# A graph layer's row gathers: two of every eight get 126 rows in place of 125

## The chip, the cores and the metric

The kernel runs on one core of a Trainium2 chip. The metric is the time of one execution on the device in microseconds (us), lower is better. A core has five engines that run their own instruction lists side by side: PE (matrix multiply), DVE (vector), ACT (scalar functions), POOL (general purpose, here the one that issues the gathers) and SP (issues plain transfers). Sixteen DMA engines move the data.

## What is computed

One message-passing layer over a graph with 12500 nodes of 64 features and 412500 edges (both directions of 200000 drawn pairs, and a loop at each node), sorted by receiver. Cut to what matters:

```python
h = relu(layernorm(x))
msg_in    = concat([h[src], h[dst], edge_attr_32], -1)      # 64 + 64 + 32
messages  = swish(msg_in @ W1 + b1) @ W2 + b2
logits    = swish(msg_in @ Wa1 + ba1) @ Wa2 + ba2
messages *= softmax(logits, axis=0)                         # over all edges
agg = segment_sum(messages, dst, num_segments=12500)
out = x + swish(concat([h, agg], -1) @ Wu1 + bu1) @ Wu2 + bu2
```

## The kernel before

**Tables.** The products of the sender's part with the two first weight matrices are made once for every node and written to a table in device memory, `ts_d`, with 128 floats (512 bytes) a node. A second table `tr_d` holds the receiver's part. An edge then needs one row of `ts_d`, by its sender's number, and no matrix product for it.

**Tiles and groups.** Edges are worked in tiles of `EP = 125`, one edge a partition, and in groups of `K = 8` tiles; there are `T = 3304` tiles and `NG = 413` groups. The senders' numbers lie in `src_full`, 128 partitions by 3304 tiles, of which partitions 125 to 127 hold zeros; `src_sb` is its first 125 partitions.

**The gather.** `load(g)` (L523) takes a buffer `gs` of 128 partitions by 8 tiles by 128 floats from a pool of seven and issues one indirect DMA on POOL for each tile (L529 to L532): partition p gets the row of `ts_d` whose number stands in `src_sb[p, tile]`. In the 131 groups in `chosen` (every third one from group 10 on, but for the last twelve) the eighth tile is not gathered; ACT copies its columns one by one out of an SBUF copy (L503). That leaves 3304 - 131 = 3173 gathers. The same `load` issues the loads of the receivers' window (`wins`, on SP), of edge features and receivers' numbers (`eo`, `dbs`, on SP), the comparison on DVE that makes a one-hot matrix (L555), and four matrix products on PE that give the receiver's and the edge's part, `pe` (L559).

**The rest of a group.** `begin(g)` (L567) adds `pe` and the gathered rows on DVE (L570; it reads all gathered tiles of the group at once) and lets ACT take the tanh (L573). `end(g)` makes the message and the logit on DVE (L583 to L594), `by_node` weighs and sums the messages by receiver with DVE (L637) and PE (L643), and `put` adds the sums to a running table (L668 to L675). The softmax is kept as a running maximum with factors.

**Order.** The loop over groups (L735) runs `begin(g)`, then `load(g + 2)`, then `end(g)`, so that gathers run two groups ahead in the list; what is marked with `pin` keeps its written order on its engine. POOL issues nothing but gathers in this loop. Each gather's list entry waits for the gather eight before it (one of eight completion counters in turn), and the first of a group also for the engines that last read its buffer.

Of the kernel before, what the change touches and what calls it, by code (L numbers as in the profile page):

```python
# [44 lines left out]
F32 = mybir.dt.float32  # L45
# [8 lines left out]
P = 128  # L54
EP = 125
# [3 lines left out]
C = 2 * U  # L59
S1 = U + 1  # L60
K = 8
# [13 lines left out]
PHASE = 1  # L75
SLOTS = (((0, 24), (24, 24)), ((48, 24), (72, 12)), ((84, 24), (108, 17)))
ROUND = 12582912.0
EPS = 1e-5
NEG = -3.0e38
BIG = 3.0e38  # L80
# [9 lines left out]
def gnn_kernel(ctx: ExitStack, tc: tile.TileContext, n_edges, x, src, src_row, dst, dst_row, first, edge,  # L90
# [73 lines left out]
    with tc.tile_pool(name="node1", bufs=1) as node1, \  # L164
# [41 lines left out]
        eps = node1.tile([P, 1], F32, name="eps")  # L206
        nc.vector.memset(eps, EPS)
        pin(nc.scalar.activation(node1.tile([P, 1], F32, name="spare"), eps, AF.Sqrt))
# [90 lines left out]
        for c, nn in chunks:  # L299
            tr = node.tile([P, CB, C], F32, name="tr")[:, :nn, :]  # L300
            for b in range(0, nn, 4):
                n = min(4, nn - b)
                pn = node_ps.tile([P, 4, C], F32, name="pn", bufs=4)
                for i in range(0, n, 2):
# [7 lines left out]
        pin(nc.scalar.dma_start(hT_d, hT))  # L312

    one_pass(tc, n_edges, locals())
    again = nc.values_load(wrong[0:1, 0:1], min_val=0, max_val=1,
                           skip_runtime_bounds_check_because="it is the outcome of a comparison")
# [76 lines left out]
def one_pass(tc, n_edges, v):  # L393
    nc = tc.nc
    NB, T, NG, NP, NT = (v[k] for k in ("NB", "T", "NG", "NP", "NT"))
    ident, iota_w, bj, dloc, src_sb, base_sb, real, unreal, far, wrong = (
        v[k] for k in ("ident", "iota_w", "bj", "dloc", "src_sb", "base_sb", "real", "unreal",
                       "far", "wrong"))
    ts_d, tr_d, bq_d, xb_d, edge, dst_row = (
        v[k] for k in ("ts_d", "tr_d", "bq_d", "xb_d", "edge", "dst_row"))  # L400
    wa2, ba2_c, w2b, wu1a, wu2h, we, gather = (
        v[k] for k in ("wa2", "ba2_c", "w2b", "wu1a", "wu2h", "we", "gather"))
# [8 lines left out]
    with ExitStack() as ctx:  # L411
# [38 lines left out]
        for w in wins:  # L450
            nc.vector.memset(w, 0.0)
            for r in range(2):
                rows = slice(WR + r * DE, WR + (r + 1) * DE)
                nc.vector.tensor_copy(w[rows, :, r, :], we[rows, None, :].to_broadcast([DE, 2, C]))
        with tc.tile_pool(name="work2", bufs=2) as work2, \
# [3 lines left out]
            pes, gss, lgs, ps_, psums, sps, pps, ees, mts, nums, cols = ({} for _ in range(11))  # L459
# [20 lines left out]
            def places(g):  # L480
# [7 lines left out]
                pin(nc.vector.tensor_scalar(near, to, 1.0 / m, 0.5 / m - 0.5, op0=ALU.mult, op1=ALU.add))  # L488
                pin(nc.vector.tensor_scalar(near, near, ROUND, None, op0=ALU.add))
                pin(nc.vector.tensor_scalar(near, near, ROUND, float(1 - m * P), op0=ALU.subtract, op1=ALU.mult))  # L490
                pin(nc.vector.scalar_tensor_tensor(to, to, float(P), near, op0=ALU.mult, op1=ALU.add))
# [13 lines left out]
            def burst(g, k):  # L505
                for i in range(EVERY):
# [6 lines left out]
                           ap=[[C, NP + WR - SHIFT], [SHIFT * C, 2], [1, C]])  # L513

            def registers(g, engine, at, base=base_sb, top=NP - 1):
                n = min(NQ, NG + (base is not base_sb) - g)
                _, regs = nc.values_load_multi_w_load_instructions(
                    base[0:1, g:g + n], engines=[engine], min_val=0, max_val=top,
                    skip_runtime_bounds_check_because=WHY)
                for i in range(n):  # L520
                    at[g + i] = regs[i]

            def load(g):  # L523

                t = g * K
                if g % NQ == 0:
                    registers(g, ENG.SP, at_sp)
                gs = gss[g] = gather.tile([P, K, C], F32, name="gs")[:EP]
                for j in range(K - (g in chosen)):  # L529
                    nc.gpsimd.indirect_dma_start(  # L530
                        out=gs[:, j, :], out_offset=None, in_=ts_d[:, :],
                        in_offset=bass.IndirectOffsetOnAxis(ap=src_sb[:, t + j:t + j + 1], axis=0))  # L532
                if g % NQ == 0:
                    n = min(NQ, NG - g) * E2
                    eo = eos[g // NQ % 2]
                    i = g // NQ % 2
                    db = dbs[i * WR:(i + 1) * WR].bitcast(I32)
                    for i in range(g, min(g + NQ, NG)):
                        e = slice((i - g) * E2, (i - g + 1) * E2)
                        ees[i] = eo[:, e], db[:, e]  # L540
                    nc.sync.dma_start(eo[WR:, :n],
                                      edge[:, g * E2:g * E2 + n])
                    for r in range(2):
                        nc.sync.dma_start(
                            db[r * R:(r + 1) * R, :n],
                            bass.AP(tensor=dst_row.tensor, offset=dst_row[r:r + 1, g * E2:].offset,
                                    ap=[[0, R], [1, n]]))
                eo, db = ees.pop(g)
                win = wins[g % WINS]
                for r in range(2):  # L550
                    nc.sync.dma_start(win[r * R:(r + 1) * R, :, r, :],
                                      tr_w[bass.ds(at_sp[g], R), :, :])
                for h in range(2):
                    e = slice(h * E2 // 2, (h + 1) * E2 // 2)
                    pin(nc.vector.tensor_scalar(eo[:WR, e], db[:, e], bj[g // NQ % 2 * WR:(g // NQ % 2 + 1) * WR, g, h:h + 1], None,  # L555
                                                op0=ALU.is_equal))
                pe = pes[g] = pre_ps.tile([P, K, C], F32, name="pe")[:EP]
                for q in range(H):
                    pin(nc.tensor.matmul(pe[:, 2 * q:2 * q + 2, :], eo[:, q * EP:(q + 1) * EP],  # L559
                                         win[:, q // 2, :, :], start=True,  # L560
                                         stop=q < H - 1 or g not in chosen))
                if g in chosen:
                    to, _ = cols[g]
                    pin(nc.vector.scalar_tensor_tensor(to, nums[g], half, to, op0=ALU.is_equal, op1=ALU.mult))
                    pin(nc.tensor.matmul(pe[:, K - 1, :], to, stack, start=False, stop=True))
# [166 lines left out]
            for g in range(AHEAD):  # L732
                load(g)
            done = 0
            for g in range(NG):  # L735
# [18 lines left out]
                if g + AHEAD < NG:  # L754
                    load(g + AHEAD)
# [382 lines left out]
```

## Time and profile before

| What | Value |
|---|---|
| median of 3 runs (lowest, highest) | 4922.53 us (4922.45, 4923.75) |
| the profiled execution's own time | 4935.06 us |
| its span, first to last instruction | 4933.3 us |
| mean granted clock of PE | 0.611 |
| gathers: number, busy, idle before them | 3173, 3853.9 us, 1020.6 us |
| DMA engines, mean busy share in mid-run | 0.33 to 0.34 |

The profile is a record of one execution. It gives each engine's busy time, and for each group of instructions (by line of the kernel) how often it ran, its mean length and what ended the idle time before it. A name behind an arrow is what the instruction waited for; "issue" is time in which it waited for nothing that the profile shows. For a gather POOL counts as busy while it prepares the transfer, not while the data move. The records of the DMA engines list every packet with its queue, size and duration; POOL's gathers are queue q0.

### The profile page before, as it was taken

The numbers are of one execution on the slowest core, as the hardware profiler recorded it, in microseconds if no ns is written. First come the engines' busy times: TensorE is split into PE (matmuls) and PEld (weight loads), VectorE is DVE, ScalarE is ACT, GpSimd is POOL, SyncE is SP. The second block draws the span as 40 slices with busy tenths as digits, with TensorE's granted clock in tenths as the row PEclk, the third lists the DMA queues.
The fourth block names the chain that finished last, engine by engine and source line by source line (L and its number), as shares of the span: only waits on it lengthen the run. The fifth ranks groups of instructions, "written<-read, shape, count | busy, mean of one in ns | idle before, by whom it ended". The sixth has DMA issues, their size and how long they took to land. (4 is left out here: it accounts for less than half of the span.)

```text
span 4933.3 us, 81829 instructions
## 1 busy us (share of the span) xinstructions
PE 2429.9 (49%) x11509; PEld 1950.7 (40%) x11509; DVE 3456.5 (70%) x9793; ACT 2214.0 (45%) x17625; POOL 3871.1 (78%) x3198
## 2 busy tenths in 40 slices
PE   5455555445544444544444544444445445444455
PEld 4343344334433333433333443333334334334344
DVE  6677777777776766766766776766767667667667
ACT  3444444444444444444444444444444444444412
POOL 4777877777777777777777777777777777777775
PEclk8666655665666665555665555566566666655655
DMA  7333333333333333333333333233333333333333
GB/s 248 76 76 83 87 75 82 89 74 83 81 75 76 71 74 76 70 75 76 69 76 76 68 76 76 68 76 76 69 76 71 74 76 70 75 76 70 75 91 81
DMA packets 377225, 396.20 MB, mean 80 GB/s; under 512 B 230333, under 2 KB 306039, under 8 KB 376290
## 3 DMA queue, kind: packets, MB, share of 16 engines
q0 software_dynamic: 253840, 206.77, 19.0%
q1 hardware_dynamic: 121458, 174.49, 14.9%
q10 hardware_dynamic: 1376, 9.67, 0.5%
q14 instruction: 457, 3.74, 0.3%
q8 instruction: 94, 1.54, 0.1%
HBM read 361.41 MB, written 25.72 MB: 78 GB/s over the span
## 5 line engine op out<-in xcount | busy, mean ns | idle before, releaser
L530 POOL DMA_INDIRECT gs<-ts_d,src_sb x3173 | 3853.9, 1215 | 1020.6 <-issue 962.4
L559 PE MATMUL pe<-wins,eo 128*125 128x256 f32 x3304 | 1524.4, 637 | 1551.2 <-DVE eo L555 1288.7
L503 ACT COPY cols<-hT 128x1 f32 x16375 | 1630.2, 189 | 754.3 <-issue 749.8
L559 PEld LDWEIGHTS pe<-wins,eo 128*125 128x125 f32 x3304 | 997.4, 319 | 1872.4 <-DVE eo L555 1375.5
L570 DVE TENSOR_TENSOR gs<-pe,gs 125x1024 f32<-125x1024 f32 (+1 forms) x413 | 487.5, 1180 | 1153.1 <-DMA gs<-ts_d,src_sb 1140.2
L573 ACT ACTIVATE pe<-gs 125x1024 f32<-125x1024 f32 x413 | 424.8, 1029 | 1768.2 <-DVE gs L570 859.2
L637 DVE TENSOR_SCALAR wt<-iota_w,dloc,p 125x40 f32<-125x40 f32 x3304 | 772.5, 364 | 1.8
L643 PE MATMUL sp<-wt,acts 125*65 125x40 f32 x6608 | 652.2, 270 | 13.2 <-DVE wt L637 9.2
L643 PEld LDWEIGHTS sp<-wt,acts 125*65 125x65 f32 x6608 | 612.5, 185 | 23.6 <-DVE wt L637 14.0
L613 PE MATMUL mt<-ident,mx 125*128 125x125 f32 x110 | 48.1, 438 | 644.7 <-DVE sums L672 608.1
L654 PEld LDWEIGHTS mt<-ss,w2u 65*128 65x128 f32 x826 | 210.7, 283 | 362.0 <-issue 235.4
L654 PE MATMUL mt<-ss,w2u 65*128 65x40 f32 x826 | 188.3, 322 | 262.8 <-DVE gm L620 199.4
L555 DVE TENSOR_SCALAR eo<-dbs,bj 64x250 f32<-64x250 int32 x826 | 303.2, 397 | 17.9 <-DMA dbs<-in_dst_row_dram 8.5
L591 DVE TENSOR_TENSOR pe<-pe,w_all 125x512 f32<-125x512 f32 x413 | 288.8, 699 | 13.7
L589 DVE SCALAR_TENSOR_TENSOR pe<-pe,gs 125x512 f32<-125x512 f32 x413 | 287.4, 696 | 10.8
L583 DVE SCALAR_TENSOR_TENSOR acts<-pe,gs 125x512 f32<-125x512 f32 x413 | 284.6, 689 | 12.8 <-issue 2.4
L594 DVE TENSOR_REDUCE lg<-pe 125x8 f32<-125x512 f32 x413 | 284.2, 688 | 10.8
L613 PEld LDWEIGHTS mt<-ident,mx 125*128 125x128 f32 x110 | 20.0, 182 | 655.8 <-issue 652.2
L675 DVE COPY stand<-nmax 64x40 f32 x826 | 217.1, 263 | 3.3
L672 DVE TENSOR_TENSOR sums<-sums,mt 64x40 f32 x606 | 114.4, 189 | 4.7 <-issue 0.4
L668 DVE SCALAR_TENSOR_TENSOR sums<-sums,scale,mt 64x40 f32 x220 | 55.8, 254 | 78.4 <-PE mt L654 59.6
L356 DVE TENSOR_SCALAR bu<-mt,w_all 64x256 f32<-64x256 f32 (+1 forms) x50 | 23.9, 478 | 92.6 <-PE mt L347 78.6
(124 smaller groups left out, 1123.2 us busy)
## 6 DMA issues: line engine op xcount, KB each, us to landing
eo<-in_edge_dram SPq DMA_DIRECT2D x103, 500.0 KB
dbs<-in_dst_row_dram SPq DMA_DIRECT2D x206, 250.0 KB
gs<-ts_d,src_sb POOLq DMA_INDIRECT x3173
wins<-tr_d SPq DMA_DIRECT2D x826, 32.0 KB
num<-in_src_row_dram SPq DMA_DIRECT2D x131, 62.5 KB
ts_d<-ts SPq DMA_DIRECT2D x5, 896.0 KB
tr_d<-tr ACTq DMA_DIRECT2D x5, 896.0 KB
hT_d<-hT ACTq DMA_DIRECT2D x1, 3136.0 KB
```

The source lines that it names most:

```text
L503: pin(nc.scalar.copy(to[:, first + i:first + i + 1], hT[:, bass.ds(regs[i], 1)]))
L530: nc.gpsimd.indirect_dma_start(out=gs[:, j, :], out_offset=None, in_=ts_d[:, :], in_offset=bass.IndirectOffsetOnAxis(ap=src_sb[:, t + j:t ...
L555: pin(nc.vector.tensor_scalar(eo[:WR, e], db[:, e], bj[g // NQ % 2 * WR:(g // NQ % 2 + 1) * WR, g, h:h + 1], None, op0=ALU.is_equal))
L559: pin(nc.tensor.matmul(pe[:, 2 * q:2 * q + 2, :], eo[:, q * EP:(q + 1) * EP], win[:, q // 2, :, :], start=True, stop=q < H - 1 or g not in ...
L570: pin(nc.vector.tensor_tensor(gss[g][:, :n, :], pes[g][:, :n, :], gss[g][:, :n, :], ALU.add))
L573: pin(nc.scalar.activation(pes[g], gss[g], AF.Tanh))
L583: pin(nc.vector.scalar_tensor_tensor(acts[g % ACTS][:, :, 0:U], th[:, :, U:C], 1.0, gs[:, :, U:C], op0=ALU.add, op1=ALU.mult))
L589: pin(nc.vector.scalar_tensor_tensor(att, th[:, :, 0:U], 1.0, gs[:, :, 0:U], op0=ALU.add, op1=ALU.mult))
L591: pin(nc.vector.tensor_tensor(att, att, wa2[:EP, None, :].to_broadcast([EP, K, U]), ALU.mult))
L637: pin(nc.vector.tensor_scalar(wt[:, j, :], iota_w[:EP, j // H, :], dloc[:, g * K + j:g * K + j + 1], p[:, k + j:k + j + 1], op0=ALU.is_equ ...
L643: pin(nc.tensor.matmul(sp, acts[g % ACTS][:, j, :], wt[:, j, :], start=j == 0, stop=j == K - 1))
L654: pin(nc.tensor.matmul(pp, w2u.rearrange("s h u -> s (h u)"), sps.pop(g), start=True, stop=True))
```

## The change

In each group the tiles j = 2 and j = 3 are gathered with 126 rows. The destination is 126 partitions of the buffer's 128, and the index list is 126 partitions of `src_full`; the 126th index is one of the zeros, so row 0 of `ts_d` goes to partition 125, which no instruction reads. The six other gathers of a group (five in a chosen one) keep their 125 rows. Everything else reads the first 125 partitions as before.

```diff
+WIDE = 126
...
-                gs = gss[g] = gather.tile([P, K, C], F32, name="gs")[:EP]
+                full = gather.tile([P, K, C], F32, name="gs")
+                gs = gss[g] = full[:EP]
                 for j in range(K - (g in chosen)):
+                    rows = WIDE if j in (2, 3) else EP
                     nc.gpsimd.indirect_dma_start(
-                        out=gs[:, j, :], out_offset=None, in_=ts_d[:, :],
-                        in_offset=bass.IndirectOffsetOnAxis(ap=src_sb[:, t + j:t + j + 1], axis=0))
+                        out=full[:rows, j, :], out_offset=None, in_=ts_d[:, :],
+                        in_offset=bass.IndirectOffsetOnAxis(ap=src_full[:rows, t + j:t + j + 1], axis=0))
```

In the changed kernel these lines stand three further down (L533 for the gather).

More of the change, by code (lines that the diff above doesn't have):

```diff
@@ L395, in one_pass @@
     NB, T, NG, NP, NT = (v[k] for k in ("NB", "T", "NG", "NP", "NT"))
-    ident, iota_w, bj, dloc, src_sb, base_sb, real, unreal, far, wrong = (
-        v[k] for k in ("ident", "iota_w", "bj", "dloc", "src_sb", "base_sb", "real", "unreal",
+    ident, iota_w, bj, dloc, src_full, base_sb, real, unreal, far, wrong = (
+        v[k] for k in ("ident", "iota_w", "bj", "dloc", "src_full", "base_sb", "real", "unreal",
                        "far", "wrong"))
```

## The prediction

> **What bounds the kernel now.** I read the page's busy shares and slices first, then the waits, then the gather's own line, then a stretch of the time line. The page's chain of work is no help here: it follows back only the last 0.1 us. Busy time by engine (share of the span, number of instructions) and POOL's row of the 40 slices:
>
> ```profile
> PE 2429.9 (49%) x11509; PEld 1950.7 (40%) x11509; DVE 3456.5 (70%) x9793; ACT 2214.0 (45%) x17625; POOL 3871.1 (78%) x3198
> ...
> POOL 4777877777777777777777777777777777777775
> ```
>
> POOL is busiest, and evenly so, yet 22% is missing. The waits say who waits for whom (us in total, times, longest):
>
> ```profile
> PEld pe L559 <- DVE eo L555: 1375.5, 381, 10.6
> ...
> DVE gs L570 <- DMA gs<-ts_d,src_sb: 1140.2, 303, 7.9
> POOL gs L530 <- issue: 962.4, 2993, 49.5
> ACT pe L573 <- DVE gs L570: 859.2, 199, 12.2
> ```
>
> PE and ACT wait for DVE, DVE waits for the gathers' data, and the gathers wait for nothing in the program ("issue"). The time line shows how (start, length, idle before it):
>
> ```profile
> 2997.52 1.21 POOL L530 DMA_INDIRECT gs<-ts_d,src_sb  x1 [0.30 <-issue]
> 2999.04 1.21 POOL L530 DMA_INDIRECT gs<-ts_d,src_sb  x1 [0.30 <-issue]
> 3000.55 1.21 POOL L530 DMA_INDIRECT gs<-ts_d,src_sb  x1 [0.30 <-issue]
> ```
>
> A metronome: 1.21 us of work and 0.30 us between two instructions, 1.52 us a gather. The line's own totals (lengths in ns, then what ended the idle time before it, in us and times, and last who waited for it):
>
> ```profile
> L530 POOL DMA_INDIRECT gs<-ts_d,src_sb x3173: 1207/1212/1726, 51.9 to 4875.7; - x199
> ...
>   issue: 962.4, 2993
> ...
>   DMA gs<-ts_d,src_sb: 7.5, 14
> ...
>   DVE gs L570: 1142.3, 304
> ```
>
> First start 51.9, last end 4875.7 + 1.2 = 4876.9, so 4825.0 us of the 4933.3 are this line: 3853.9 busy and some 971 between instructions (its 1020.6 idle less 49.5 before the first). Only 14 gathers ever waited for a landing (7.5 us in all), so free buffers and slow transfers are not the limit. Before lie 51.9 us, behind 56.4 us, and the change touches neither. The time of this kernel is 3173 gathers times 1.52 us plus 108 us.
>
> **The change, part by part.** Instruction counts and waits are the same on all five engines; on PE, DVE, ACT and SP the lists agree row for row. The two gathers j = 2 and 3 of each of the 413 groups get 126 rows. No chosen group drops them (those drop j = 7), so 826 gathers change and 2347 do not.
>
> Edits that cost nothing: partition 125 of the gather buffer is written and read by nobody. The index array already holds 128 partitions and was already loaded whole, so no load is added. The 512 bytes more are 826 x 512 B = 0.42 MB on a queue that moves 206.77 MB, in DMA engines busy a third of the time; without that cover they would be 826 times the 27 ns that a 512-byte packet takes in the trace, 22 us over all engines. No wait is added, so nothing new queues behind a gather. An earlier landing of tiles 2 and 3 is worth nothing either, since DVE's addition (L570) reads all tiles of the group, and the last ones keep 125 rows.
>
> What can cost or pay is POOL's own time on a 126-row gather. No row of this trace has one, so I look at what a 125-row gather leaves behind:
>
> ```profile
> q0 software_dynamic: 253840, 206.77, 19.0%
> ```
>
> That is 253840/3173 = exactly 80 packets a gather. By size the trace's records have 15 of 4096 B, 5 of 512 B, 33 of 32 B and 27 of 4 B for each. The 20 large ones are 5 x (3 x 8 + 1) = 125 rows: five of the 16 engines get 25 rows each. The small ones are, for the 11 other engines, 3 x 8 + 1 = 25 entries of 4 B, plus 16 completions. So every one of 16 rings is filled 26 entries deep, 11 of them with dummies. The split is even, into five, and five is the largest number up to 16 that divides 125. Read the same way 126 goes to 14 engines with 9 rows, and the rings are 10 deep: 16 levels fewer.
>
> [...]
>
> What is a level worth? POOL's other instructions bound it (count, busy us, mean ns):
>
> ```profile
> L840 POOL TENSOR_TENSOR gs<-gs,eo 128x512 f32<-128x512 f32 x6 | 7.6, 1270 | 24.4 <-ACT mt L827 20.2 <-DVE gs L835 2.5 <-issue 1.7
> ...
> L141 POOL IOTA iota_p<- 32x1 f32 x4 | 0.5, 127 | 0.1
> ...
> masks.py:197 POOL MEMSET ident<- 128x128 f32 x1 | 0.2, 205 | 0.3 <-POOLq L1130 0.3
> ...
> L1130 POOL MEMSET const-float32-1.0<- 128x1 f32 x1 | 0.1, 102 | 0.0
> ```
>
> Least: a level is one element column of a memset, (205 - 102)/127 = 0.81 ns, and 16 levels are 13 ns. Most: an instruction's fixed part is the 127 ns of the smallest iota and all the rest is levels: (1212 - 127) x 16/26 = 668 ns. [...] I take 179 ns; it is nearest to work that POOL really does, and it leaves 1.03 us a wide gather. The 0.30 us between instructions I leave as it is.
>
> Sum, on the profiled execution's own span: 826 x 0.179 = 148 us less, 4933.3 - 148 = 4785. That execution took 4935.06 us (span and 1.8 around it) against a median of 4922.53, so in terms of the median 4785 x 4922.53/4933.3 = **4775 us**, 3.0% faster. The stall does not reappear within that: a group's period falls from 8 x 1.517 = 12.1 us (less in chosen groups) by 0.36, and the stretch 2000 to 3000 us has DVE 692.56 busy, so DVE would stand at 71%.
>
> [...]
>
> **The rivals.** (B) Slower: engines that carry data are what costs, not levels. Place: the same 826 instructions, whose live engines go from 5 to 14. Bounds for one live engine: 10 ns, from the first packets of a gather's 16 rings, which start within some 0.16 us of each other, and (1212 - 127)/5 = 217 ns if nothing else costs. It decides from 179/9 = 20 ns an engine, where it eats the gain. Its geometric middle, 47 ns, gives 9 x 47 - 179 = +244 ns, x 826 = +201 us, **5123 us**. For it: data packets rise from 20 to 28, and a dummy needs no index. Against it: the dummies are written all the same, in the same depth, as if 16 rings were filled side by side.
>
> (C) Nothing: rows cost, one by one, however they are split (or the split stays as it is and the change does no more than it says). 1212/125 = 9.7 ns a row, x 826 = +8 us, **4931 us**, +0.16%. For it: the simplest reading of a loop over an index list. Against it: 291 of 416 entries are not rows.
>
> (D) The gain nears the upper end, 668 ns, and another engine becomes the bound. 826 x 0.668 = 552 us would leave 4371; DVE's 3456.5 us busy would then be 79% and its waits for PE and ACT would show. I hold anything below 4640 (342 ns saved, half the most) at 8 in 100.
>
> **How the numbers follow.** A 0.46 (0.08 of it below 4640), B 0.42 (0.10 of it above 5130), C 0.12 (a measurement of this kernel tells 0.2% from no change; most of C is within that, 0.09, the rest slower). The time is A's, 4775; A's own range is 4640 to 4900. As the signs share the chance, the range spans 4640 to 5130 and leaves out 0.18. Faster 0.46, within 0.2% 0.09, slower 0.45.
>
> **What would show it.** Split: q0 should have 2347 x 80 + 826 x 48 = 227408 packets (14 x 2 data, 2 x 2 dummies, 16 completions); near 253840 the split is another and A and B both fall. Price: in the gather's line the median stays 1212 and 826 instructions, two adjacent ones in every eight, stand at some 1030 ns (A), 1450 (B) or 1222 (C). End: first start near 51.9 and a tail near 56 us; if the gathers then wait for something other than "issue", POOL has stopped being the bound and D holds. Wrong would be a gap that moves off 0.30 us, or unchanged gathers that change too.

## The result, and the profile after

The changed kernel takes 4744.97 us (median of 4 runs, 4742.4 to 4745.24) against 4922.49 us before (4 runs): a ratio of 0.9638, 95% interval 0.9621 to 0.9654. It is 177.5 us faster; forecast were 4775 us.

The page of the changed kernel, its busy times, POOL's row of slices and POOL's transfer queue (packets, MB, share of 16 engines):

```profile
PE 2412.1 (51%) x11509; PEld 1935.5 (41%) x11509; DVE 3391.0 (71%) x9793; ACT 2202.3 (46%) x17625; POOL 3682.4 (78%) x3198
...
POOL 4777777777777777777777777777777777777775
...
q0 software_dynamic: 227408, 206.34, 19.4%
```

Every engine has the same number of instructions as before, and POOL has 188.7 us less to do. Queue q0 has exactly the 227408 packets that follow from 14 equal shares of 9 rows. By size, with 80 packets for each of the 2347 other gathers, they leave 14 of 4096 B, 14 of 512 B, 2 of 32 B and 18 of 4 B for each wide one. The gathers' own line (lengths in ns, first and last start, then what ended the idle time before it):

```profile
L533 POOL DMA_INDIRECT gs<-ts_d,src_sb x3173: 992/1209/1550, 52.2 to 4685.9; - x199
...
  issue: 952.1, 2961
...
  DMA gs<-ts_d,src_sb: 15.1, 40
```

The first gather starts where it did (52.2 us) and the tail is as long (last end 4687.1, span 4742.9: 55.8 us). Between them lie 4635.0 us, 190.0 less than before. The time line of a group in mid-run (start, length, idle before it):

```profile
2994.23 1.21 POOL L533 DMA_INDIRECT gs<-ts_d,src_sb  x1 [0.30 <-issue]
2995.74 1.00 POOL L533 DMA_INDIRECT gs<-ts_d,src_sb  x1 [0.30 <-issue]
2997.05 1.00 POOL L533 DMA_INDIRECT gs<-ts_d,src_sb  x1 [0.30 <-issue]
2998.35 1.21 POOL L533 DMA_INDIRECT gs<-ts_d,src_sb  x1 [0.30 <-issue]
```

Two adjacent gathers are 0.21 us shorter, the gap stays at 0.30 us, and still nothing but POOL itself sets the pace. By tile the medians are 996 ns for j = 2 and 3 and 1209 ns for the six others. And who waits for whom (us in total, times, longest):

```profile
PEld pe L562 <- DVE eo L558: 1283.1, 378, 11.1
...
DVE gs L573 <- DMA gs<-ts_d,src_sb: 1006.7, 289, 8.6
POOL gs L533 <- issue: 952.1, 2961, 49.8
ACT pe L576 <- DVE gs L573: 829.1, 212, 11.7
```

Beside the lines of before, the two waits on DVE and the wait on the gathers' data have all shrunk, by 30 to 134 us, as is to be expected when POOL delivers sooner; none has taken the place of another.

### The profile page after: what moved, and what is told of

Its sections match the earlier page's. It is cut to its first block, busy times and chain, and to the rows that moved or that the text cites. A ratio compares the mean times of both kernels' runs of the same rounds, so it can differ in the third digit from the quotient of the medians.

```text
span 4742.9 us, 81829 instructions
## 1 busy us (share of the span) xinstructions
PE 2412.1 (51%) x11509; PEld 1935.5 (41%) x11509; DVE 3391.0 (71%) x9793; ACT 2202.3 (46%) x17625; POOL 3682.4 (78%) x3198
## 3 DMA queue, kind: packets, MB, share of 16 engines
q0 software_dynamic: 227408, 206.34, 19.4%
## 5 line engine op out<-in xcount | busy, mean ns | idle before, releaser
L533 POOL DMA_INDIRECT gs<-ts_d,src_sb x3173 | 3665.2, 1155 | 1019.6 <-issue 952.1
L646 PE MATMUL sp<-wt,acts 125*65 125x40 f32 x6608 | 641.2, 267 | 12.9 <-DVE wt L640 10.6
L646 PEld LDWEIGHTS sp<-wt,acts 125*65 125x65 f32 x6608 | 600.1, 182 | 24.2 <-DVE wt L640 19.9
L594 DVE TENSOR_TENSOR pe<-pe,w_all 125x512 f32<-125x512 f32 x413 | 288.7, 699 | 13.7
L558 DVE TENSOR_SCALAR eo<-dbs,bj 64x250 f32<-64x250 int32 x826 | 281.0, 370 | 17.8 <-DMA dbs<-in_dst_row_dram 8.5
L678 DVE COPY stand<-nmax 64x40 f32 x826 | 185.4, 224 | 3.3
L675 DVE TENSOR_TENSOR sums<-sums,mt 64x40 f32 x606 | 114.1, 188 | 4.6 <-PE mt L657 0.6
```

What stands on the lines that cost most here:

```text
L533: nc.gpsimd.indirect_dma_start(out=full[:rows, j, :], out_offset=None, in_=ts_d[:, :], in_offset=bass.IndirectOffsetOnAxis(ap=src_full[:ro ...
L594: pin(nc.vector.tensor_tensor(att, att, wa2[:EP, None, :].to_broadcast([EP, K, U]), ALU.mult))
L646: pin(nc.tensor.matmul(sp, acts[g % ACTS][:, j, :], wt[:, j, :], start=j == 0, stop=j == K - 1))
```

## The experiments

The words are the prediction's, and they are a reading of packet counts. A gather of 125 rows leaves 15 packets of 4096 B, 5 of 512 B, 33 of 32 B and 27 of 4 B, and the counter that it completes on is stepped 16 times (at the changed kernel's first gather, one of 125 rows, 11 times within 0.17 us, and five times 0.65 us and more after those). Read as 16 rings, one for each DMA engine: five hold 25 rows each, eight to a large packet; 11 hold as many dummies of 4 B, eight to a packet of 32 B; each ends in one entry more. Depth is counted below without that last entry, and an engine with data is an equal share of the rows. The records name neither an engine nor an entry; measured are the packets, the steps and POOL's times. The theory: POOL pays for each entry of the deepest ring (a level). Its rivals: it pays for dummies, for packets, for rows, or for engines that carry data; or a shape costs something by what stands beside it. All ratios are against the kernel before on the same chip.

### Sixteen row counts in one run (e1_shapes)

```diff
+SHAPES = (125, 126, 128, 127, 124, 122, 120, 112, 110, 100, 96, 80, 64, 50, 25, 16)
...
+    junk = const.tile([P, C], F32, name="junk")
...
+                if 8 <= g < NG - 13:
+                    rows = SHAPES[g % len(SHAPES)]
+                    nc.gpsimd.indirect_dma_start(
+                        out=v["junk"][:rows], out_offset=None, in_=ts_d[:, :],
+                        in_offset=bass.IndirectOffsetOnAxis(ap=v["src_full"][:rows, t:t + 1], axis=0))
```

> The kernel before, with one gather more in most groups, into a buffer that nobody reads; its row count goes in turn through 125, 126, 128, 127, 124, 122, 120, 112, 110, 100, 96, 80, 64, 50, 25, 16. Only the length of these gathers on POOL is of interest (the time grows by some 380 gathers). Depth theory (13.5 ns for each entry of the deepest ring, 216 ns/16, whoever carries data): 128 and 120 rows 982 ns, 112 969, 110 and 100 1009, 96 955, 80, 50 and 25 all 942, 64 928, 16 888, 124 1293, 122 1698, 127 2589. Dummy theory (0.84 ns for each dummy entry, 216/257, no price on depth): 128, 112, 96, 80, 64 and 16 all 981, 120 988, 110 1023, 100 1031, 50 1006, 25 1027, 124 1293, 122 1698, 127 2581. Packet theory (108 ns for every started eight entries of a ring): everything with up to 8 entries 888, 110 and 100 996, 124 1212, 122 1644, 127 2508. Row theory (9.7 ns a row): 16 rows 155, 64 rows 621, 127 rows 1231.

The scheduler moved these extra gathers forward (they run from 140 to 2235 us), and most (306 of 392) wait for the one before to land, as they write one buffer. So this run's time (6199.11 us) says nothing; the lengths do. POOL's time line over five of them, which by their order in the list take 126, 128, 127, 124 and 122 rows:

```profile
1050.19 1.00 POOL L537 DMA_INDIRECT junk<-ts_d,src_sb  x1 [2.42 <-DMA junk<-ts_d,src_sb]
1053.52 0.96 POOL L537 DMA_INDIRECT junk<-ts_d,src_sb  x1 [2.33 <-DMA junk<-ts_d,src_sb]
1056.41 2.55 POOL L537 DMA_INDIRECT junk<-ts_d,src_sb  x1 [1.93 <-DMA junk<-ts_d,src_sb]
1064.58 1.30 POOL L537 DMA_INDIRECT junk<-ts_d,src_sb  x1 [5.61 <-DMA junk<-ts_d,src_sb]
1068.47 1.67 POOL L537 DMA_INDIRECT junk<-ts_d,src_sb  x1 [2.60 <-DMA junk<-ts_d,src_sb]
```

127 rows take 2.55 us where 126 take 1.00 and 128 take 0.96. And two pairs that matter below, of 110 and 100 rows, then of 25 and 50:

```profile
1003.95 1.01 POOL L537 DMA_INDIRECT junk<-ts_d,src_sb  x1 [0.30 <-issue]
1007.47 1.01 POOL L537 DMA_INDIRECT junk<-ts_d,src_sb  x1 [2.51 <-DMA junk<-ts_d,src_sb]
...
1030.61 0.95 POOL L537 DMA_INDIRECT junk<-ts_d,src_sb  x1 [1.79 <-DMA junk<-ts_d,src_sb]
...
1289.60 0.94 POOL L537 DMA_INDIRECT junk<-ts_d,src_sb  x1 [0.31 <-issue]
```

The medians of the 24 or 25 gathers of each shape, with the number of equal shares, worked out as the largest divisor up to 16, and the rows in each share:

| rows | shares | rows in each | ns |
|---|---|---|---|
| 127 | 1 | 127 | 2556 |
| 122 | 2 | 61 | 1671 |
| 124 | 4 | 31 | 1298 |
| 125 | 5 | 25 | 1214.5 |
| 110 | 11 | 10 | 1012 |
| 100 | 10 | 10 | 1012 |
| 126 | 14 | 9 | 999 |
| 120 | 15 | 8 | 991 |
| 50 | 10 | 5 | 950 |
| 25 | 5 | 5 | 951 |
| 128 | 16 | 8 | 958 |
| 112 | 16 | 7 | 943 |
| 96 | 16 | 6 | 932 |
| 80 | 16 | 5 | 919 |
| 64 | 16 | 4 | 912 |
| 16 | 16 | 1 | 870 |

The trace's packet count agrees with the two middle columns: with them, at eight rows or dummies a packet at most, dummies to the same depth in the rings without rows and one packet more at the end of each ring, the 392 extra gathers leave 24480 packets, and queue q0 has 278320 in this run, 24480 more than the 253840 of before.

The column "rows in each" orders the whole upper part. A straight line through the ten shapes below 16 shares is 883 ns + 13.1 ns for each row in a share, and no shape is further from it than 14 ns. Four pairs decide:

- 50 and 25 rows have the same depth, but 10 and 5 shares and twice the rows: 950 and 951 ns. An engine with data, a row and a dummy (30 and 55 of them) have no price of their own that shows.
- 110 and 100 rows: 1012 both, with 11 and 10 shares.
- 64 and 16 rows have no dummies at all, and one packet of data a share each: 912 and 870. By the dummy theory (981) and the packet theory (888) they would be equal.
- 124 rows need as many packets a ring as 125 (four, at eight entries each) and one row fewer, and take 84 ns more.

So dummies, packets, rows and live engines fall, and depth stands. What the depth theory missed is a second line: with 16 shares the price of a level is nearly the same (12.2 ns), but the constant is lower (859 ns); 128 rows take 33 ns less than 120 at the same depth of 8. One thing the runs leave open: all rings of a gather have the same depth, so a price for each level and a sixteenth of it for each entry of all 16 rings, whatever the entry holds, are the same sum here.

### All gathers with 126 rows (e2_all126)

```diff
-                    rows = WIDE if j in (2, 3) else EP
+                    rows = WIDE
```

> All gathers with 126 rows. If POOL stays the bound: 3173 x (0.996 + 0.304) + 108 = 4233 us of span, 4224 us in terms of the median. If another engine takes over (DVE has 3391 us busy, 8.2 us a group, against a gather period of 10.4 us): 4300 to 4450 us, and gathers that wait for something other than issue.

4253.56 us, ratio 0.8625 (0.861 to 0.8639). The gathers' line of this run:

```profile
L533 POOL DMA_INDIRECT gs<-ts_d,src_sb x3173: 992/996/1449, 50.6 to 4184.4; - x199
...
  issue: 876.7, 2879
```

Their median is 996 ns, the profiled span is 4242.6 us against the 4233 of the sum, and the waits are still "issue": 3.84 times as many wide gathers (3173 against 826) bring 3.80 times as much (0.1375 of the time against 0.0362), so POOL stays the bound.

### All gathers with 128 rows (e3_all128)

```diff
-                    rows = WIDE if j in (2, 3) else EP
+                    rows = P
```

> All gathers with 128 rows, three of them to unused partitions. Depth theory: 8 entries a ring, 982 ns, 3173 x (0.982 + 0.304) + 108 = 4189 us of span, 4180 by the median. Packet theory: 888 ns, 3890 us, if no other engine takes over. Row theory: 998 ns or more, not faster than with 126 rows.

4093.31 us, ratio 0.83 (0.8286 to 0.8314). Busy times of this run and its gathers' line:

```profile
PE 2389.3 (58%) x11509; PEld 1923.0 (47%) x11509; DVE 3340.5 (82%) x9793; ACT 2199.8 (54%) x17625; POOL 3021.6 (74%) x3198
```

```profile
L533 POOL DMA_INDIRECT gs<-ts_d,src_sb x3173: 938/944/1422, 51.8 to 4024.2; - x199
...
  issue: 890.6, 2922
```

944 ns, 38 less than the depth theory's 982: 24 of them showed in the run of shapes too (958), where they go with the lower constant of 16 shares. The other 14 ns, by which the same shape was longer among mixed shapes, are not explained. The row theory is wrong in sign, the packet theory is 56 ns off. DVE is now busy for more of the span than POOL (82% and 74%), and yet the gathers wait for "issue" 2922 times: POOL's 0.30 us between two gathers are not counted as busy, and it remains the bound.

### Wide gathers that are not neighbours (e4_apart)

```diff
-                    rows = WIDE if j in (2, 3) else EP
+                    rows = WIDE if j in (0, 4) else EP
```

> The first and the fifth tile with 126 rows in place of the third and the fourth: no two wide gathers follow each other. If each gather's price is its own: 996 ns each and 4745 us again. If a change of the shape costs or the second of a pair profits: wide gathers of another length than 996 ns, or 125-row gathers after a wide one longer than 1209 ns, and a time that differs by 826 times that.

4752.07 us in one run, beside a median of 4932.1 before on this chip: 0.9635, the change's ratio again. Its time line over two wide gathers:

```profile
3002.78 1.00 POOL L533 DMA_INDIRECT gs<-ts_d,src_sb  x1 [0.30 <-issue]
3004.09 1.22 POOL L533 DMA_INDIRECT gs<-ts_d,src_sb  x1 [0.30 <-issue]
3005.61 1.21 POOL L533 DMA_INDIRECT gs<-ts_d,src_sb  x1 [0.30 <-issue]
3007.13 1.00 POOL L533 DMA_INDIRECT gs<-ts_d,src_sb  x1 [0.30 <-issue]
```

The medians are 999 ns (wide) and 1212 ns (125 rows). That the third and the fourth tile were chosen, and that they are neighbours, plays no part that shows. Here 125 rows have the 1212 ns of before, not the 1209 of the changed kernel's profile; as the wide ones are 3 ns longer too, those 3 ns lie between executions and not in the change.

### Tiles of 128 edges (e5_tile128)

```diff
-EP = 125
+EP = 128
...
-SLOTS = (((0, 24), (24, 24)), ((48, 24), (72, 12)), ((84, 24), (108, 17)))
+SLOTS = (((0, 24), (24, 24)), ((48, 24), (72, 12)), ((84, 24), (108, 20)))
...
-                    rows = WIDE if j in (2, 3) else EP
+                    rows = P
```

> Tiles of 128 edges instead of 125 throughout (3224 tiles, 403 groups, so some 3096 gathers of 128 rows, no unused rows). Depth theory with what the last runs showed (944 ns a 128-row gather, 305 between two): 3096 x 1.249 + 114 = 3981 us, 0.81 of before. If DVE, 82% busy in the run with 128-row gathers, becomes the bound: above 4040, and gathers that wait for something other than issue.

3994.33 us, ratio 0.8099 (0.8085 to 0.8112), the fastest version here. The gathers' line:

```profile
L533 POOL DMA_INDIRECT gs<-ts_d,src_sb x3097: 941/947/1436, 50.9 to 3934.3; - x194
...
  issue: 877.7, 2878
```

76 gathers fewer at 1.25 us each are 95 us of the 99 between this version and the one with 128 rows in all gathers (4093.31 us); the bound is still POOL.

### 127 rows in the change's place (e6_wide127)

```diff
-WIDE = 126
+WIDE = 127
```

> The change with 127 in place of 126 rows in the third and fourth tile. Depth theory: 127 is prime, so one ring takes all rows and is 127 entries deep; 2556 ns a gather as in the run of shapes, 826 x (2.556 - 1.212) = +1110 us, about 6040 us. A theory in which more rows or more engines with data make the gather shorter: 996 ns or less, 4745 us or less.

6048.78 us in one run, 1117 us slower than the 4931.9 us of before on its chip. Its time line:

```profile
3003.70 1.21 POOL L533 DMA_INDIRECT gs<-ts_d,src_sb  x1 [0.30 <-issue]
3005.22 2.57 POOL L533 DMA_INDIRECT gs<-ts_d,src_sb  x1 [0.31 <-issue]
3008.09 2.55 POOL L533 DMA_INDIRECT gs<-ts_d,src_sb  x1 [0.30 <-issue]
3010.94 1.22 POOL L533 DMA_INDIRECT gs<-ts_d,src_sb  x1 [0.30 <-issue]
```

One row more than the change makes the gather 2.57 times as long (median 2557 ns). 127 has no divisor up to 16 but 1, and q0 has 412432 packets, exactly those of 2347 gathers with 80 each and 826 with 272 each, which is the count for all 127 rows in one share. The depth theory's 6040 us holds within 9 us. A price for each row (9.7 ns) would add 16 us, and a price for each engine with data would give a saving, since by that count one engine carries data here in place of five. A small rest does not follow from the depth: the two 125-row gathers behind each such pair take 1217 ns instead of 1212.

## Why the prediction was right

**The bound.** "3173 gathers times 1.52 us plus 108 us" held: of the 190.4 us that the span lost, 188.7 are POOL's busy time in this line and 1.3 its gaps.

**The split.** 14 shares of 9 rows: 227408 packets forecast and found. The largest divisor up to 16 agrees with the other packet counts too: 127 rows in one share (412432), 128 in 16 (101536, 32 for each gather), and the sixteen shapes in their sum.

**The price of a level** was the mis-sized term: the sum took 179 ns for 16 levels, 11.2 ns each, an assumption of the author's that no run shows; 13.5 ns each were found in place (1212 - 996 = 216 ns over 16 levels), 13.1 over the ten shapes below 16 shares. So a wide gather takes 996 ns and not 1033, and the sum 826 x 0.216 = 178 us is the 177.5 us between the medians; forecast were 148. That POOL's time follows the levels, the rows in a share, is what the experiments show, from the lowest depths on (with 16 shares 870 ns at one row each, 912 at four). That the price was right to a sixth is luck: the bounds were 13 and 668 ns for 16 levels (4912 to 4371 us), nothing in the trace of before gave the value between them, and what POOL does for one level no run here shows.

**The free edits** were free: the gap between gathers stayed at 0.30 us, only 40 gathers waited for a landing (15.1 us), and DVE stands at the 71% that was worked out.

**The rivals.** (B) priced an engine with data at 10 to 217 ns; 25 and 50 rows, in 5 and 10 shares, put it at nothing (951 and 950 ns). It had been given almost the chance of the right case, since nothing in the trace of before could tell levels from engines: a single shape was to be seen. (C), 9.7 ns a row, falls by the same pair and by 127 rows. (D) did not come: even with 128 rows in all gathers and DVE at 82% no other engine became the bound.

**The profiled execution** of before was 12.5 us above its median (4935.06 and 4922.53), that of the changed kernel on it (4744.76). That is why the two spans differ by 190 us and the medians by 178: the 125-row gathers at the six other tiles average 1215.0 ns in the one and 1210.6 in the other, 2347 x 4.4 ns = 10 us.

## What to carry to other kernels

Where POOL issues gathers back to back, count the packets that one gather leaves in its queue before choosing the number of rows: the size and number of the packets told here into how many equal shares the rows went, and the rows in each share set POOL's time (13.1 ns each below 16 shares, 12.2 with 16). Among the counts tried here, 128 rows take 0.26 us less than 125, so rows to unused partitions more than pay for themselves, while 127 rows more than double the gather. An engine that shows 74% busy can still be the bound when its gaps are fixed (0.30 us here): look whether the waits before its instructions name anyone.

## What the runs showed of the hardware that was not expected

- An indirect gather of 125 rows leaves 33 packets of 32 B and 27 of 4 B beside its 20 of data, one of 126 rows 2 and 18 beside 28. All 16 rings filled to the same depth give these counts. The dummies of that reading cost POOL nothing that the depth does not: 100 and 110 rows, with 60 and 50 of them, take 1012 ns both.
- With fewer than 16 shares POOL's time for a gather is a straight line in rows per share from 5 to 127 (883 ns + 13.1 ns each, no shape off by more than 14 ns), and the number of rows makes no difference beside it (25 and 50 rows: 951 and 950 ns).
- With 16 shares there is a further saving of 33 ns at the same depth (958 ns for 128 rows against 991 for 120, 8 rows a share). Its cause was not tried.
- The length of the gathers shows on DVE as well. With the same instructions DVE is busy for 3456.5 us before, 3391.0 with the change, 3340.5 with 128 rows in all gathers and 4228.1 with 127 in two tiles. Copies and tensor-scalar operations stretch: the copy of 64x40 (L675, L678 in the changed kernels) takes 263, 224, 202 and 531 ns on average, while the product of two 125x512 tensors (L591, L594) has 699 ns in all four. The cause was not tried. In these runs POOL was the bound, so this cost no time of its own that shows.
